# Three edits in an attention stage: a shorter second search update, side work tied to places of a turn, and unread matmuls where a place is empty

## The chip, the cores and the metric

The kernel runs on one core of a Trainium2 chip. The core has TensorE (matmuls; PE in the profile, PEld for its weight loads), VectorE (DVE), ScalarE (ACT), GpSimd (POOL) and SyncE (SP, which here only issues transfers). The engines run side by side and wait for each other through semaphores; each works its own instructions in the order in which the program gave them. The metric is the device time of one execution, in microseconds (us).

## The reference, cut to what matters

The program is two layers of a small vision network on four images of 256 channels and 32 x 32 = 1024 positions. Layer 0 is an attention block and a mixture of experts, layer 1 a selective scan and a mixture of experts. The change touches the attention block alone:

```
qkv  = conv1x1(x, qkv_w, qkv_b)          # 8 heads, 16 + 16 + 32 channels
attn = einsum(q, k) * SCALE              # 1024 x 1024 scores per head
k    = floor(N * mean(sigmoid(...)))     # one number for the whole batch
attn = where(rank of a score in its row < k, attn, -inf)
out  = einsum(v, softmax(attn))
pe   = depthwise 3x3 convolution of v
x    = x + conv1x1(out + pe, proj_w, proj_b)
```

Only the k largest scores of a row take part in the softmax, so the kernel must find for each of the 4 x 8 x 1024 rows the value of its k-th largest score. It does so by a search: it guesses a threshold, counts how many scores lie under it, and moves the threshold.

## The kernel before, in words

**Halves and turns.** The work is cut into 64 halves: 4 images, 2 groups of 4 heads, 4 pairs of query tiles, 2 tiles of 128 queries. One half is 128 queries for four heads, so four rows of 1024 scores in each partition. Half i enters in turn i, and a half stays in work for some eight turns, so each turn works on several halves at once: h0 is the one that enters, h1 entered one turn before, h2 two, h3 three; `pair` is two finished halves that go through the softmax together. Nothing reorders the work: the instructions go to each engine exactly as `turn(i)` writes them.

**One turn.** In the order of the code: TensorE computes the second half of h0's scores (`scores(1)`, L526) and ScalarE copies the four score tiles out of PSUM (`take`, L534). TensorE computes scores again, transposed and with the dropped ones pushed down, for two key tiles of the pair (`weights(q)`, L637 and L642). VectorE reads out the seven largest scores under h3's threshold (`window`, L551 and L554; two rows now, two later) and does the first search update (`update`, L592 to L616), for h1 and h2. ScalarE counts all four rows of h0 at its first guess (L500). Place 0. ScalarE takes exponentials (`exps`, L650), TensorE multiplies with the values and with ones (`sums`, L660). ScalarE and VectorE count h1 (L500 and L504). Place 1. TensorE does `weights(q + 1)`. VectorE does the second search update, for h0 and h1. Both count h2 a last time. GpSimd writes h3's mask, four instructions `dr` (L584), of which the first is told to wait for the second update, and then `verify` (L573 to L578). Place 2. Exponentials again; h0 is counted. Place 3. `start(i + 1)` computes the first half of the next half's scores (`scores(0)`, L526). h1 is counted. TensorE does the second `sums`. Place 4.

**Buffers.** Score tiles and transposed score tiles share three PSUM buffers of two banks. The scores of a half lie in SBUF in two of eight buffers `s_n`, so ScalarE's copies of a new half wait until the mask `dr` of the half four turns older has read them. All side work of TensorE shares one PSUM bank, `m`, with one buffer (`bank`).

**Side work and places.** Everything else of an image goes into five places of a turn, the calls `beside(i)`: the q and k of the next head group with their statistics and first guesses (`Group.steps`, 12 chunks), the values (`values`, 4 chunks a group), the convolution and its projection (`rest`: 4 chunks `vp`, 4 x 3 chunks of three convolution products, 4 chunks `pp`) and the last projection (`finish`, 4 chunks). Each is a generator. It yields True when a chunk of TensorE's work is issued, and the place is then closed; the instruction that empties the bank `m` is issued when the generator is next called, and the next chunk follows in the same place. `todo` holds for each generator the turn from which it may run, the turn by which it must be done, and whether a chunk is open. An open one goes on first, otherwise the one that is due first. `due(i)`, called by `start(i)`, runs whatever must be done by turn i, at once, ahead of `scores(0)`. The `rest` of an image also issues on GpSimd: a memset of `vpad` and, ahead of the first convolution chunk of each channel half, nine products `diag` (L450), which the convolution's matmuls (L455) load as weights. The last chunk of a group is the moments `mo` (L381, L382); behind them stands a square root on GpSimd (`sd`, L391), and VectorE then writes the guesses (L400 to L405). `rest` loads the image a second time by one SyncE transfer of 1 MB (`x_res`, L463).

Image b has turns 16 b to 16 b + 15, and its side work runs from turn 16 b + 5 to 16 b + 23.

Of the kernel before, what the change touches and what calls it, by code (L numbers as in the profile page):

```python
# [17 lines left out]
ALU = mybir.AluOpType  # L18
# [34 lines left out]
def metaformer(ctx: ExitStack, tc: tile.TileContext, t: dict, out: bass.AP):  # L53
    nc = tc.nc

    cons = ctx.enter_context(tc.tile_pool(name="cons", bufs=1))
    ident = cons.tile([P, P], F32, tag="ident", name="ident")
# [5 lines left out]
    first = cons.tile([P, E], F32, tag="first", name="first")  # L63
# [117 lines left out]
    with ExitStack() as st:  # L181
        wp = st.enter_context(tc.tile_pool(name="a_w", bufs=1))

        wqk = load_rows(wp, "wqk", 4 * P)
# [36 lines left out]
        with tc.tile_pool(name="a_ln", bufs=2) as lp, \  # L221
                tc.tile_pool(name="a_lnp", bufs=4, space=PSUM) as psl:
            g1 = load(lp, "g1", [P, CT, P], t["g1"].rearrange("(c p) o -> p c o", p=P))
            for b in range(B):
# [3 lines left out]
                for h in range(NHALF):  # L228
                    gp = psl.tile([P, HALF], F32, tag="m", name="gp")
                    for c in range(CT):  # L230
                        nc.tensor.matmul(gp, g1[:, c, :], xn[b][:, c, ts(h, HALF)],
                                         start=(c == 0), stop=(c == CT - 1))
# [5 lines left out]
                    i = b * NHALF + h  # L238
# [66 lines left out]
        def bank(name):  # L305

            return ps1.tile([P, HALF], F32, tag="m", name=name)
# [283 lines left out]

        def update():  # L592

# [4 lines left out]
            br = bracket.rearrange("p e k n j -> p e k (n j)")  # L598
            t, u = st_[:, 0], st_[:, 1]
# [8 lines left out]
            fr = p2.tile([P, R], F32, tag="fr", name="fr", bufs=1)  # L608
            nc.vector.scalar_tensor_tensor(fr, br[:, 0, 1, :], aim, dd[:, 1, :], ALU.subtract, ALU.mult)
            nc.vector.tensor_tensor(fr, fr, dd[:, 0, :], ALU.mult)  # L610
            nc.vector.tensor_tensor(fr, br[:, 0, 0, :], fr, ALU.subtract)
            low = p2.tile([P, R], F32, tag="low", name="low", bufs=1)
# [66 lines left out]

        todo = [[0, 0, groups[0, 0].steps(), False], [0, 0, images[0].values(0), False]]  # L680
        for b in range(B):
            i = b * PER
            todo.append([i + 5, i + 8, groups[b, 1].steps(), False])
            todo.append([i + 8, i + 13, images[b].values(1), False])
            if b + 1 < B:
                todo.append([i + 13, i + 16, groups[b + 1, 0].steps(), False])
                todo.append([i + 16, i + 21, images[b + 1].values(0), False])
            todo.append([i + 9, i + 20, images[b].rest(), False])
            todo.append([i + 21, i + 23, images[b].finish(), False])

        def beside(i):

            while True:
                ready = [w for w in todo if w[0] <= i]
                if not ready:
                    return
                w = next((w for w in ready if w[3]), None) or min(ready, key=lambda w: w[1])
                try:
                    w[3] = next(w[2])
                except StopIteration:  # L700
                    todo.remove(w)
                    w[3] = False
                if w[3]:
                    return
# [11 lines left out]
        def turn(i):  # L716
# [16 lines left out]
            if half(1) or half(2):  # L733
                to_u(slice(0, 2), FIRST_DVE[1])
                update()
            if h2:
# [3 lines left out]
            if h0:  # L740
                h0.count(4, h0.at_guess)
            beside(i)
            if pair:
# [6 lines left out]
            if h1:  # L750
                h1.count(FIRST_DVE[0], h1.at_state)
            beside(i)
            if pair:
# [13 lines left out]
            beside(i)  # L767
# [4 lines left out]
            beside(i)  # L772
            if i + 1 < len(order):
# [3 lines left out]
            if pair:  # L777
                pair.sums(q + 1)
            beside(i)

# [830 lines left out]
```

## Time and profile before

| | us |
|---|---|
| median of 3 runs (lowest, highest) | 4864.83 (4861.07, 4874.88) |
| profiled execution, and its span | 4900.55, 4898.8 |
| attention stage within the span | about 130 to 2120 |
| busy there: TensorE, VectorE, ScalarE, GpSimd | 1481.34, 1606.06, 1621.85, 915.86 |
| granted TensorE clock there, of full speed | 0.76 |

Below, a turn runs from ScalarE's first copy of a half's scores (L534, four copies a turn, 256 in all) to that of the next. Turn 0 starts at 140.2 us in the span. The turns of the second image and the first ones of the third, which repeat from image to image almost to a tenth:

| turns | starts at | length of each, us |
|---|---|---|
| 21 to 24 | 711.0 | 27.4, 31.0, 36.5, 31.1 |
| 25 to 28 | 837.1 | 31.6, 31.2, 35.6, 31.7 |
| 29, 30 | 967.2 | 30.4, 28.3 |
| 31, 32 | 1025.8 | 29.2, 29.5 |
| 33 to 36 | 1084.4 | 25.2, 26.7, 26.1, 26.7 |

Turns 17 to 20, 33 to 36, 49 to 52 and 62, 63 hold no side work at all.

How to read the profile's rows: a line of the timeline is the start in us from the span's start, the duration, the engine, the line of the kernel, the operation, the tile written and the tiles read, the shapes, and how many alike follow each other; in brackets how long the engine had been idle and what ended that. A line of groups ends with the total, the mean in ns and the idle time ahead. A matmul of f32 data shows as two entries.

### The profile page before, as it was taken

What the parts mean: (1) busy time and instruction counts of PE and PEld (TensorE: products, weight loads), DVE (VectorE), ACT (ScalarE), POOL (GpSimd) and SP (SyncE); (2) the same over time, 40 slices, a digit from 0 to 9 for tenths busy, and PEclk for the clock granted to TensorE, in tenths of its full rate; (3) what the DMA queues carried; (4) which work ended last, traced back from release to release, by engine and by line L of the source; (5) the groups of instructions that cost most, each with busy time, mean ns of one, the idle gap of its engine ahead of it and who ended that gap; (6) DMA issues with size and microseconds to landing.
All of it is one profiled execution on the core that took longest, in us unless ns stands there. A gap on an engine that the chain in (4) does not pass through costs nothing.

```text
span 4898.8 us, 51450 instructions
## 1 busy us (share of the span) xinstructions
PE 4004.6 (82%) x18714; PEld 2228.5 (45%) x18714; DVE 3255.5 (66%) x5263; ACT 2894.4 (59%) x3813; POOL 1405.0 (29%) x1126
## 2 busy tenths in 40 slices
PE   7378777877787777689999799989989994599993
PEld 4143434343434343356666333434433432488882
DVE  2687897789778887732223799999999995111212
ACT  3788898788878978522111666677666762122221
POOL 0244444545445454510000122222222223200004
PEclk8578767877797678778999899999999997799995
DMA  3000000000000000010000223323323334334433
GB/s 128 0 1 9 1 1 1 9 1 1 1 9 1 1 1 9 1 36 1 0 1 3 78 92 112 103 87 112 104 86 112 112 111 146 118 115 121 119 109 107
DMA packets 128616, 264.86 MB, mean 54 GB/s; under 512 B 29017, under 2 KB 77282, under 8 KB 127586
## 3 DMA queue, kind: packets, MB, share of 16 engines
q1 hardware_dynamic: 118144, 243.15, 15.3%
q0 software_dynamic: 6144, 16.79, 1.1%
q8 instruction: 150, 2.46, 0.2%
q10 hardware_dynamic: 4066, 1.55, 0.1%
q14 instruction: 112, 0.92, 0.1%
HBM read 224.74 MB, written 36.70 MB: 53 GB/s over the span
## 4 chain that ended last, share of the span: by engine, by line
PE 29%; DVE 19%; issue 3%; SPq 2%; ACT 2%; DMA 1%; POOL 0%; another core or an unknown queue 0%; ACTq 0%; DVEq 0%; POOLq 0%
PE hp L1505 6%; PE yp L1511 6%; PE y L1012 5%; PE hp L1005 5%; DVE h L1284 4%; DVE h L1269 4%; DVE h L1260 4%; PE hp L1255 3%; DVE yc L1294 2%; SPq L1478 2%; DVE h L1278 1%; PE y L1295 1%; PE hp L1288 1%; ACT da_c L1242 0%; PE y L173 0%
## 5 line engine op out<-in xcount | busy, mean ns | idle before, releaser
L584 POOL TENSOR_SCALAR dr<-s_n,last 128x1024 bf16<-128x1024 f32 x256 | 724.6, 2848 | 955.2 <-DVE state L616 598.7
L1240 POOL TENSOR_TENSOR uu<-dx,bb 128x1024 f32<-128x1024 f32 x128 | 317.4, 2480 | 1521.3 <-issue 807.9
L500 ACT ACTIVATE junk_a<-s_n,state 128x1024 int8<-128x1024 f32 x448 | 514.1, 1148 | 21.7 <-DVE state L616 11.7
L1255 PE MATMUL hp<-h,ident 128*128 128x512 f32 x1024 | 496.9, 608 | 27.3 <-DVE h L1278 19.0
L1242 ACT ACTIVATE da_c<-delta,a_log 128x1024 f32<-128x1024 f32 x128 | 270.0, 2109 | 307.1 <-DVE h L1284 307.1
L504 DVE TENSOR_SCALAR_CACHE_REDUCE junk_v<-s_n,state 128x1024 int8<-128x1024 f32 x320 | 408.6, 1277 | 8.0
L1507 ACT ACTIVATE hid<-hp,b 128x256 f32<-128x256 f32 x312 | 145.1, 473 | 415.4 <-PE hp L1505 415.4
L534 ACT COPY s_n<-sp 128x1024 f32<-128x1024 f32 x256 | 246.4, 1014 | 227.0 <-PE sp L526 166.8
L551 DVE SCALAR_TENSOR_TENSOR w<-s_n,win 128x1024 f32<-128x1024 f32 x256 | 359.3, 1403 | 5.5
L1014 DVE SCALAR_TENSOR_TENSOR acc<-y,tk_comb,acc 128x256 f32<-128x256 f32 x256 | 121.0, 484 | 356.0 <-PE y L1012 352.1
L660 PE MATMUL o_ps<-ex,vT 128*32 128x256 f32 x2048 | 274.1, 490 | 83.8 <-ACT ex L650 81.0
L1514 DVE TENSOR_TENSOR ys<-yp,b2e 128x512 f32<-128x512 f32 x39 | 27.0, 692 | 467.4 <-PE yp L1511 467.4
L1255 PEld LDWEIGHTS hp<-h,ident 128*128 128x128 f32 x1024 | 191.3, 193 | 304.3 <-issue 202.5
L554 DVE MAX8 win<-w 128x8 f32<-128x1024 f32 x256 | 314.5, 1228 | 8.8
L1255 PE MATMUL hp<-h,twice 128*128 128x512 f32 x512 | 258.8, 625 | 64.1 <-DVE h L1260 40.6
L500 ACT ACTIVATE junk_a<-s_n,guess 128x1024 int8<-128x1024 f32 x256 | 295.0, 1152 | 6.2
L1260 DVE TENSOR_TENSOR_SCAN h<-da,uu 128x1024 f32<-128x1024 f32 x128 | 290.1, 2266 | 3.6 <-ACT da L1248 3.6
L1284 DVE TENSOR_TENSOR_SCAN h<-da_c,uu 128x1024 f32<-128x1024 f32 x128 | 292.3, 2284 | 0.0
L1007 ACT ACTIVATE hid<-hp,b 128x512 f32<-128x512 f32 x128 | 88.0, 687 | 345.6 <-PE hp L1005 344.8
L1269 DVE TENSOR_TENSOR_SCAN h<-da,uu 128x1024 f32<-128x1024 f32 x128 | 289.9, 2264 | 0.0
L1505 PE MATMUL hp<-xe,w 128*128 128x256 f32 x1248 | 280.8, 383 | 7.5 <-DVE xe L1498 7.5
L650 ACT ACTIVATE ex<-sT 128x1024 f32<-128x1024 f32 x256 | 246.4, 1012 | 63.1 <-PE sT L642 62.7
(480 smaller groups left out, 8147.7 us busy)
## 6 DMA issues: line engine op xcount, KB each, us to landing
bb<-bc_d SPq DMA_DIRECT2D x128, 512.0 KB, 4.8
cb<-bc_d SPq DMA_DIRECT2D x128, 512.0 KB, 4.0
w<-in_w SPq DMA_DIRECT2D x47, 1024.0 KB, 5.0
slots_x<-zeros SPq DMA_DIRECT2D x1, 9984.0 KB, 32.4
xs<-slots_x SPq DMA_DIRECT2D x39, 256.0 KB, 3.1
slots_y<-ys SPq DMA_DIRECT2D x39, 256.0 KB, 2.4
b2e<-in_b SPq DMA_DIRECT2D x39, 128.0 KB, 3.8
x_in<-in_x SPq DMA_DIRECT2D x4, 1024.0 KB, 7.9
```

Source lines behind the costliest of these rows:

```text
L500: nc.scalar.activation(junk, self.row(r), AF.Sign, bias=thr, scale=-1.0, accum_out=u)
L504: nc.vector.tensor_scalar(junk, self.row(r), thr, None, ALU.is_lt, ALU.add, accum_out=u)
L551: nc.vector.scalar_tensor_tensor(w, self.row(r), self.win[:, r, 0:1], self.row(r), ALU.is_gt if r < LAST_DVE else ALU.is_ge, ALU.subtract, ...
L554: nc.vector.max(out=self.win[:, r, 1:], in_=w)
L584: ins = nc.gpsimd.tensor_scalar(dr, self.row(r), self.last[:, r : r + 1], None, ALU.is_lt)
L1240: nc.gpsimd.tensor_tensor(self.uu[:, 0], self.prep.dx[:, c], self.bb, ALU.mult)
L1255: nc.tensor.matmul(self.hp[h], ident if eye is None else eye, view[:, ts(h, HW // NHALF), :], start=first, stop=False)
L1260: nc.vector.tensor_tensor_scan(rows.rearrange("p r w -> p (r w)"), self.da, self.uu[:, 0], 0.0, ALU.mult, ALU.add)
L1269: nc.vector.tensor_tensor_scan(hs[:, ::-1], self.da[:, ::-1], self.uu[:, 0][:, ::-1], 0.0, ALU.mult, ALU.add)
L1284: nc.vector.tensor_tensor_scan(hs, self.da_c, self.uu[:, 1], 0.0, ALU.mult, ALU.add)
L1505: nc.tensor.matmul(hp[:, f % 2], w1[:, c, ts(f, P)], xe[:, c], start=(c == 0), stop=(c == CT - 1))
L1511: nc.tensor.matmul(yp[:, a], hid[:, f, ts(a, P)], w2e[:, f, :], start=(f == 0), stop=(f == NF - 1))
```

## The change

First, `update` gets an argument. The call near the start of a turn passes `stay=True` and does what it did. The call in the middle passes `stay=False`: it leaves out the two comparisons that find the rows whose count is already near the aim (L613, L615) and the predicated copy that spares those rows (L616), and writes the new threshold of every row by the subtraction.

Second, a start is now given in places, five to a turn, and a generator may be limited to some places: the groups to places 1 to 4, from place 2 of one turn earlier than before; the convolution and its projection (`rest`) to places 1 and 3. A chunk that is open goes on in any place.

Third, where a place of the first 64 turns has nothing to start, `keep_awake` issues matmuls of the identity with a weight matrix into a fresh tile of the bank `m`: two in place 0, one elsewhere. Nothing reads them.

```diff
-        def update():
+        def update(stay):
...
+            if not stay:
+                return nc.vector.tensor_tensor(t, br[:, 0, 0, :], fr, ALU.subtract)
             nc.vector.tensor_tensor(fr, br[:, 0, 0, :], fr, ALU.subtract)
...
-        todo = [[0, 0, groups[0, 0].steps(), False], [0, 0, images[0].values(0), False]]
+        PLACES = 5
+        todo = []
+
+        def plan(first, needed, steps, places=range(PLACES)):
+            todo.append([first, needed, steps, False, places])
+
+        plan(0, 0, groups[0, 0].steps())
+        plan(0, 0, images[0].values(0))
         for b in range(B):
             i = b * PER
-            todo.append([i + 5, i + 8, groups[b, 1].steps(), False])
-            todo.append([i + 8, i + 13, images[b].values(1), False])
+            plan((i + 4) * PLACES + 2, i + 8, groups[b, 1].steps(), (1, 2, 3, 4))
+            plan((i + 8) * PLACES, i + 13, images[b].values(1))
             if b + 1 < B:
-                todo.append([i + 13, i + 16, groups[b + 1, 0].steps(), False])
-                todo.append([i + 16, i + 21, images[b + 1].values(0), False])
-            todo.append([i + 9, i + 20, images[b].rest(), False])
-            todo.append([i + 21, i + 23, images[b].finish(), False])
-
-        def beside(i):
+                plan((i + 12) * PLACES + 2, i + 16, groups[b + 1, 0].steps(), (1, 2, 3, 4))
+                plan((i + 16) * PLACES, i + 21, images[b + 1].values(0))
+            plan((i + 9) * PLACES, i + 20, images[b].rest(), (1, 3))
+            plan((i + 21) * PLACES, i + 23, images[b].finish())
+
+        def keep_awake(count):
+            junk = bank("junk_p")
+            for _ in range(count):
+                nc.tensor.matmul(junk, ident, wqk[:, 0, :], start=True, stop=True)
+
+        def beside(i, place=None):
             while True:
-                ready = [w for w in todo if w[0] <= i]
-                if not ready:
+                ready = [w for w in todo if w[0] <= i * PLACES + (place or 0) and (place is None or place in w[4])]
+                w = next((w for w in todo if w[3]), None) or min(ready, key=lambda w: w[1], default=None)
+                if w is None:
+                    if place is not None and i < len(order):
+                        keep_awake(2 if place == 0 else 1)
                     return
-                w = next((w for w in ready if w[3]), None) or min(ready, key=lambda w: w[1])
...
-                update()
+                update(stay=True)
...
-            beside(i)
+            beside(i, 0)
...
-            after = update() if h0 or h1 else None
+            after = update(stay=False) if h0 or h1 else None
```

The other four calls of `beside` pass 1, 2, 3 and 4. Read through by hand, the new rules give for the turns 21 to 36 these chunks; `e` is the emptying of the bank by ScalarE or VectorE, J1 and J2 are unread products, and `due` is what `start` runs ahead of `scores(0)`:

| turn | place 0 | 1 | 2 | 3 | 4 |
|---|---|---|---|---|---|
| 21 | e, finish | e, finish | e, finish | e, finish | e, qp |
| 22 | e, J2 | ktp | e, ktp | e, mp | e, mq |
| 23 | e, J2 | mq | e, mo | mo | due: sd, guess, vtp; vtp |
| 24 | e, vtp | vtp | e, J1 | J1 | J1 |
| 25, 26 | J2 | vp | e, J1 | vp | e, J1 |
| 27 | J2 | conv | conv | conv | e, J1 |
| 28 | J2 | conv | conv | conv | e, qp |
| 29 | e, J2 | qp | e, qp | e, qp | e, ktp |
| 30 | e, J2 | ktp | e, mp | e, mq | e, mq |
| 31 | e, J2 | mo | mo | sd | due: guess, diag, conv; conv |
| 32 | conv | e, conv | conv | conv | e, vtp |
| 33 | vtp | e, pp | e, vtp | vtp | e, J1 |
| 34 | J2 | pp | e, J1 | pp | e, J1 |
| 35 | J2 | pp | e, J1 | J1 | J1 |
| 36 | J2 | J1 | qp | e, qp | e, qp |

The other images are alike, except that the last has no next group: its twelve convolution chunks stand in turns 59 to 62, in places 1 to 3. In all 177 unread products are issued.

More of the change, by code (lines that the diff above doesn't have):

```diff
@@ L751, in turn @@
                 h1.count(FIRST_DVE[0], h1.at_state)
-            beside(i)
+            beside(i, 1)
             if pair:
@@ L766, in turn @@
                     pairs[h3.i // 2] = Pair(halves[h3.i - 1 : h3.i + 1], images[h3.b])
-            beside(i)
+            beside(i, 2)
             if pair:
@@ L771, in turn @@
                 h0.count(FIRST_DVE[1], h0.at_state)
-            beside(i)
+            beside(i, 3)
             if i + 1 < len(order):
@@ L778, in turn @@
                 pair.sums(q + 1)
-            beside(i)
+            beside(i, 4)
         with tc.manual_schedule():
```

## The prediction

> **What bounds the kernel now.** First the stage view of 130 to 2120 us (columns: PE, PEld, DVE, ACT and POOL busy, then granted clock): no engine is full, and ScalarE (1621.85 of 1990) and VectorE (1606.06) are nearly equal. So waits decide, and ScalarE's waits come next (waiter, what it waited for, total, times, longest).
>
> ```profile
> 130.00:2120.00 1990.00, 1481.34 (x10559) 760.66 (x10559) 1606.06 (x3393) 1621.85 (x2414) 915.86 (x725) 0.76 0.02 5
> ...
> ACT s_n L534 <- PE sp L526: 166.8, 55, 7.0
> ACT ex L650 <- PE sT L642: 62.7, 24, 6.9
> ACT s_n L534 <- POOL dr L584: 58.0, 32, 3.7
> ```
>
> The largest wait is for scores that stand on TensorE behind side work: in turn 27, three convolution products ahead of `scores(1)`.
>
> ```profile
> 901.55 2.84 PE L455 MATMUL ap__6501<-vpad,diag 128*128 128x512 f32 x6
> ...
> 904.32 1.14 PE L526 MATMUL sp<-k__5278,q 16*128 16x512 f32 x8
> ...
> 905.49 2.84 ACT L534 COPY s_n<-sp 128x1024 f32<-128x1024 f32 x3 [4.61 <-PE sp L526]
> ```
>
> Turn 34 has no side work. There the mask holds ScalarE: the update ends, four `dr` run for 11.3 us, and the copies wait for the last. `scores(1)` is done by then.
>
> ```profile
> 1127.89 0.17 DVE L616 COPY_PREDICATED state<-move,fr 128x8 f32<-128x8 int32 x1
> ...
> 1128.26 11.30 POOL L584 TENSOR_SCALAR dr<-s_n,last 128x1024 bf16<-128x1024 f32 x4 [13.24 <-DVE state L616]
> ...
> 1134.46 2.08 PE L526 MATMUL sp<-k__7127,q 16*128 16x512 f32 x4
> ...
> 1136.33 1.90 ACT L534 COPY s_n<-sp 128x1024 f32<-128x1024 f32 x2
> ...
> 1139.59 1.93 ACT L534 COPY s_n<-sp 128x1024 f32<-128x1024 f32 x2 [1.35 <-POOL dr L584]
> ```
>
> Last, two places where GpSimd's order counts. `diag` and `sd` that are issued after the mask start only behind it and `verify`:
>
> ```profile
> 870.92 6.95 POOL L450 TENSOR_SCALAR diag<-ident,pe_w 128x128 f32<-128x128 f32 x9
> ...
> 871.58 2.84 PE L455 MATMUL ap__6310<-vpad,diag 128*128 128x512 f32 x6 [1.07 <-POOL diag L450]
> ...
> 804.23 5.44 POOL L391 TENSOR_TENSOR sd<-sd,half 128x32 f32<-128x32 f32 x1
> ...
> 809.70 0.25 DVE L400 SCALAR_TENSOR_TENSOR guess<-sd,z,mo 128x32 f32<-128x32 f32 x1 [6.97 <-POOL sd L391]
> ```
>
> **ScalarE's own turn** is the yardstick: in turn 34, 26.7 us less its 1.92 us wait for `dr`, so 24.8 us without side work. I add emptyings (0.67 us each with a 0.07 gap) and waits. As a check, turn 27 before: 24.8 + two emptyings 1.5 + waits 4.6 and 1.7, and 3.3 at the next turn's first copy: 35.9, against 35.6.
>
> **The shorter update** takes away L613, L615 and L616, 261 + 229 + 175 ns; at turn 34 the end of the update moves from 1128.06 to 1127.45, 0.6 us. Over 65 turns that is 40 us of VectorE, and on the path only where ScalarE waits for `dr`: the empty turns, 26.2 on average, become 25.6. Elsewhere ScalarE or TensorE ends last. Over turns 18 to 20, 34 to 36 and 50 to 52 it is -3.4 net of the projection now put there. Ends: 0, and 0.6 in all turns, -40; I stay near the first, since 32 short waits for `dr` are all there is to shorten.
>
> **The convolution's four turns** (25 to 28 and their like) lose the chunks ahead of `scores`. What remains is place 4: ScalarE empties the bank last in its turn, and the next product waits for that and stands ahead of `scores(1)`, which the second copy waits for. The wait is the product, plus 1.15 for the scores, plus 0.15 of handing over, less 1.0 for the first copy. An unread product has the shape of a convolution product: 2.84 / 3 = 0.95 us at full clock, and 1.5 where those ran cold (4.54 for three at 914.01). So 1.25 us with J1 and some 2.8 with a qp chunk (1.95); cold, 2.8 with J1. TensorE's queue in turn 27: fixed work 10.5 us at full clock, three chunks 8.5, J2 and J1 2.9, 22 in a turn of 27, so the chunks in places 1 to 3 hide behind counts (3.8, 3.7 and 5.0 us of ScalarE) but leave `scores(1)` 0.6 late. Turns 25 to 28 become 26.3, 27.7, 27.5 and 27.4: 108.9 for 130.1. For the four images 437 for 514.6: -78.
>
> **Turns 4 to 8 and 21 to 24.** The first fall from 145.1 to 136. In the later three sets mp and mq move one turn forward, so VectorE's 4.3 us wait for mp goes, but `sd` still stands behind the mask: mask 11.3, `verify` 1.7, `sd` 5.4, guess 1.4 and then VectorE's counts and windows to the first update, 10.5 us, which ScalarE's count waits for. 123 for 126 each. Together -17. Turns 13 and 14 and their like: +1.2 each, +4, the qp and ktp of place 4.
>
> **The collision in turns 15, 31 and 47** is the step against the change. Before, `sd` stood in place 1, ahead of the mask. Now it stands in place 3, and `due` puts the guess, the second channel half's `diag` and a convolution chunk ahead of `scores(0)`. From the start of turn 31: second update ends at 19.3, mask 30.6, `verify` 32.3, `sd` 37.8, first `diag` 38.5. TensorE, idle since 22, starts the convolution cold, 5.1 us, then `scores(0)`, first copy at 45.4 instead of about 27; then `sums`, the chunk in place 4, `scores(1)`: second copy at 52, counts at 55. From there before's turn 24 needed 24.3 us to its end. So turns 31 and 32 take 80 instead of 58.6, and turn 33, with vtp behind an emptying and a pp chunk, 29.2 instead of 25.2: +25 a time, three times, +75. Neither `diag` nor `sd` has other cover; the last image has no such turn. Ends: 0, if the chunk hid as in turn 25, and 35, if turn 32 also runs cold throughout.
>
> **Moved and free.** `vpad`'s memset (2.02 us) stays ahead of the mask with GpSimd idle; without that cover the mask would be 2 late. The `x_res` transfer starts when the convolution ends, turn 32, and its first reader is in turn 33, place 2, over 20 us later; SyncE has nothing else queued. J products in places 0 to 3 hide under the exponentials and counts: in turn 34 TensorE is busy 19 of 26.7 us; uncovered, each would cost 1 to 1.5. In empty turns J1 of place 4 is hidden: `sums` end at 1134.5, and the second copy needs `scores(1)` at 1137.3. Turns 0 to 3, 61, 62 and the tail, where two pp chunks spill: about 0.
>
> **Sum:** -78 - 17 + 4 + 75 - 3 = -19 us on the profiled 4900.6, so 4881.6. That execution is 0.7% above the median of the runs; the same 0.4% off 4864.8 gives 4846.
>
> **The clock.** In the window 1112.1 to 1125.7 the granted clock was 0.50 although TensorE was busy for 8.59 us and its longest gap was 2.9. [...] By the rows, turn 26 with 25.2 us busy of 31.2 ran at 1.00, so I take the filled turns as warm.
>
> **Rivals.** (1) *Place 4 costs more*, the slower case. 33 turns have ScalarE empty the bank in place 4 with a product behind it. Cold throughout, each costs 1.5 us more: +50, 4896. For: the half clock in turn 34, and turn 28's cold chunk (4.2 us). Against: turn 26. It decides from 19 / 33 = 0.6 us a turn, and is measurable from 1.0. (2) *No collision*: the convolution of turn 31 hides, three times 20 us come back, 4786. For: in turn 25 the chunk waited 1 us for `diag`. Against: there no `sd` stood between. (3) *The two cancel*: a collision of 31 each, or convolution turns of 28.5, brings 4865. For: two large terms of opposite sign. Also possible: the change doesn't raise the clock at all; then it is rival 1.
>
> **How the numbers follow.** Forecast (-15 to -50, own range 4815 to 4850) 0.40; rival 1 0.20; rival 2 0.13; rival 3 0.27. 0.3%, 15 us, is what a measurement of this kernel can tell. Faster is the forecast and rival 2, 0.53; same 0.27; slower 0.20. The range 4798 to 4888 leaves out rival 2 and the worse half of rival 1's chance, bounded by the collision's ends (15 to 31 each) and 0.8 us a turn in place 4.
>
> **What would show it.** Turns 27 and its like near 27.5 us; ScalarE's wait for sp well under 167 outside turns 16, 32 and 48, and there 15 to 25 us each, behind `diag`; waits for `dr` falling; granted clock of the stage near 0.9 or more; 65 fewer L613 entries. I am wrong if the collision is far from 25, or if place 4 costs over 2 us with one unread product.

## The result, and the profile after

The changed kernel takes **4888.85 us** (median of 4 runs, 4884.46 to 4891.17) against 4865.09 (4 runs, 4861.07 to 4874.88) for the kernel before on the same chip: a ratio of 1.0045, 95% interval 1.0027 to 1.0062. It is slower by 24 us, where I forecast 19 faster with a range of 4798 to 4888. The sign is wrong and the time lies just outside the range.

The profiled execution after took 4891.17 us (span 4889.5). Its attention stage, from the first copy of scores to the first instruction of the next stage, takes 1983.1 us. The kernel before takes 1962.2 there in the execution shown above and 1964.9 in a second one, so the loss of 18 to 21 us lies in this stage. (The spans of the two first profiles differ the other way round, 4898.8 to 4889.5. That comes from later stages, some 30 us longer in that one execution of the kernel before and not in its second one, which took 4871.29 us.)

First the stage view of 130 to 2120 us of the kernel after (busy PE, PEld, DVE, ACT, POOL, granted clock), then its waits (waiter, what it waited for, total, times, longest).

```profile
130.00:2120.00 1990.00, 1545.25 (x10843) 749.51 (x10843) 1551.14 (x3184) 1620.44 (x2408) 924.00 (x724) 0.81 0.01 3
...
ACT s_n L534 <- PE sp L526: 221.6, 76, 16.9
...
DVE guess L400 <- POOL sd L391: 69.0, 7, 11.0
...
ACT s_n L534 <- POOL dr L584: 11.7, 9, 3.6
```

TensorE is busier by 64 us, VectorE less busy by 55, and the granted clock went from 0.76 to 0.81. ScalarE hardly waits for the mask any more (58.0 before, 11.7 now), but waits longer for scores (166.8 before, 221.6 now): one wait has taken the place of another. VectorE's wait for `sd` has doubled (33.0 before).

The convolution's turns did what they should. The start of turn 27 in the timeline of the kernel after:

```profile
908.11 0.67 ACT L443 ACTIVATE vpad<-vp,bv_col 128x512 f32<-128x512 f32 x1
908.68 1.00 ACT L534 COPY s_n<-sp 128x1024 f32<-128x1024 f32 x1
...
908.83 1.13 PE L705 MATMUL junk_p<-wqk,ident 128*128 128x512 f32 x2 [1.25 <-ACT vpad L443]
...
909.89 1.14 PE L526 MATMUL sp<-k__5008,q 16*128 16x512 f32 x8
...
911.06 2.84 ACT L534 COPY s_n<-sp 128x1024 f32<-128x1024 f32 x3 [1.39 <-PE sp L526]
```

Three convolution products and a wait of 4.61 us stood here before. Now ScalarE empties the bank, one unread product follows, and the second copy waits 1.39 us.

The collision came as described: `sd` and the nine `diag` behind the mask and `verify`, TensorE idle for 13 us, and the copy of turn 32 behind all of it.

```profile
1041.78 11.30 POOL L584 TENSOR_SCALAR dr<-s_n,last 128x1024 bf16<-128x1024 f32 x4 [13.96 <-DVE state L612]
...
1054.63 5.44 POOL L391 TENSOR_TENSOR sd<-sd,half 128x32 f32<-128x32 f32 x1
1060.06 6.04 POOL L450 TENSOR_SCALAR diag<-ident,pe_w 128x128 f32<-128x128 f32 x9
1060.10 0.36 DVE L400 SCALAR_TENSOR_TENSOR guess<-sd,z,mo 128x32 f32<-128x32 f32 x1 [10.99 <-POOL sd L391]
...
1060.73 5.42 PE L455 MATMUL ap__7745<-vpad,diag 128*128 128x512 f32 x6 [13.03 <-POOL diag L450]
...
1066.08 1.14 PE L526 MATMUL sp<-k__7011,q 16*128 16x512 f32 x8
...
1067.31 1.01 ACT L534 COPY s_n<-sp 128x1024 f32<-128x1024 f32 x1 [16.85 <-PE sp L526]
```

In an empty turn the kernel before waited for `dr`. Turn 36 of the kernel after shows what is there now: the sums end, the unread product of place 4 runs, then the scores, and the second copy waits 2.02 us for them.

```profile
1180.65 0.99 ACT L534 COPY s_n<-sp 128x1024 f32<-128x1024 f32 x1
...
1180.89 0.61 PE L662 MATMUL o_ps<-ex,ones 128*32 128x256 f32 x8
...
1181.44 1.12 PE L705 MATMUL junk_p<-wqk,ident 128*128 128x512 f32 x2
...
1182.49 1.14 PE L526 MATMUL sp<-k__7011,q 16*128 16x512 f32 x8
1183.67 2.84 ACT L534 COPY s_n<-sp 128x1024 f32<-128x1024 f32 x3 [2.02 <-PE sp L526]
```

The lengths of the turns, summed by groups, place the loss (us; measured is after less the first profile of before):

| turns | before, two profiles | after | predicted | measured |
|---|---|---|---|---|
| 0 to 3 | 78.6, 78.6 | 75.8 | about 0 | -2.8 |
| 4 to 8 | 145.1, 145.1 | 148.9 | -9 | +3.8 |
| 21 to 24 and their like | 376.8, 378.1 | 386.5 | -8 | +9.7 |
| convolution, four times four | 514.6, 513.9 | 443.7 | -78 | -70.9 |
| 13, 14 and their like | 176.0, 177.5 | 177.8 | +4 | +1.8 |
| 15 to 17 and their like | 252.3, 251.2 | 315.6 | +75 | +63.3 |
| 18 to 20 and their like | 238.0, 238.6 | 252.7 | -3 | +14.7 |
| 61 to the end of the stage | 180.8, 181.9 | 182.2 | about 0 | +1.4 |
| sum | 1962.2, 1964.9 | 1983.1 | -19 | +20.9 |

The two large terms hold to within 12 us each and together give -8, where they were predicted to give -3. They belong together: half of the convolution's chunks and its projection left the four turns for turns 31 to 35 and their like, so the -71 holds work that has moved. The miss of 40 is in the small ones: the groups' turns (4 to 8, 21 to 24) by 30, turns 18 to 20 by 18; all other lines give back 8.

### The profile page after: what moved, and what is told of

It is laid out like the page before. It is cut to its first block, busy times and chain, and to the rows that moved or that the text cites. A ratio compares the mean times of both kernels' runs of the same rounds, so it can differ in the third digit from the quotient of the medians.

```text
span 4889.5 us, 51952 instructions
## 1 busy us (share of the span) xinstructions
PE 4075.9 (83%) x19068; PEld 2220.5 (45%) x19068; DVE 3207.5 (66%) x5068; ACT 2897.3 (59%) x3813; POOL 1414.4 (29%) x1126
## 5 line engine op out<-in xcount | busy, mean ns | idle before, releaser
L1525 ACT ACTIVATE hid<-hp,b 128x256 f32<-128x256 f32 x312 | 145.1, 473 | 415.3 <-PE hp L1523 415.3
L534 ACT COPY s_n<-sp 128x1024 f32<-128x1024 f32 x256 | 246.8, 1015 | 241.9 <-PE sp L526 221.6
L551 DVE SCALAR_TENSOR_TENSOR w<-s_n,win 128x1024 f32<-128x1024 f32 x256 | 348.6, 1362 | 5.4
L705 PE MATMUL junk_p<-wqk,ident 128*128 128x512 f32 x354 | 257.2, 846 | 87.5 <-ACT vpad L443 18.0
L662 PE MATMUL o_ps<-ex,vT 128*32 128x256 f32 x2048 | 237.3, 448 | 74.4 <-ACT ex L652 68.4
```

The costliest lines, as they stand in the source:

```text
L551: nc.vector.scalar_tensor_tensor(w, self.row(r), self.win[:, r, 0:1], self.row(r), ALU.is_gt if r < LAST_DVE else ALU.is_ge, ALU.subtract, ...
```

## The experiments

After the two traces my **theory** was: the collision eats what the convolution's places bring; the unread products bring little, because those in place 4 stand ahead of scores; the shorter update brings little. The **rivals**: the unread products are the loss by themselves; the shorter update is worth much more than its waits show and something hides it; the groups' new places, not the collision, are the loss. Ratios are always to the kernel before on the same chip. Its median was 4874.12 us in the first batch, 4893.97 in the second and 4873.95 in the third, so ratios, and not times, are compared across batches. Times in brackets are ranges, ratios in brackets 95% intervals.

### The kernel before once more

No edit, one profile, to learn how much one profiled execution differs from the next.

> The kernel before once more, for a second profiled execution. If the extra 28 us behind the attention stage in the first one (627, 106 and 98 us for three stretches in which the changed kernel took 616, 100 and 87) belong to that execution alone, this one has the shorter stretches, with attention again at 1962 us. If they belong to the kernel, it has the longer ones again.

Measured: 4871.29 us, attention stage 1964.9, every group of turns within 1.5 us of the first profile. What the table above shows beyond that is the change.

### The shorter second update alone

The kernel before with the new argument of `update`, and nothing else.

```diff
-        def update():
+        def update(stay):
...
+            if not stay:
+                return nc.vector.tensor_tensor(t, br[:, 0, 0, :], fr, ALU.subtract)
...
-                update()
+                update(stay=True)
...
-            after = update() if h0 or h1 else None
+            after = update(stay=False) if h0 or h1 else None
```

> The kernel before with the shorter second update alone. Theory that VectorE is off the path but for the mask: only turns in which ScalarE waits for dr gain, up to 0.6 us each, some 20 to 30 turns, so -10 to -18 us (4848 to 4855), and the waits of the copies for dr fall from 58 to about 40 us. Rival, VectorE bounds every turn: 65 turns at 0.6 us, -40 us (4825). Rival, nothing: the next limit takes it over, within 5 us of before.

Measured: 4850.02 us (4848.51 to 4856.14), ratio 0.9955 [0.9941, 0.9968]: **24 us faster**, more than the theory's 10 to 18 and less than the rival's 40. Two waits of ScalarE in the second profile of the kernel before:

```profile
ACT s_n L534 <- PE sp L526: 162.7, 54, 7.4
...
ACT s_n L534 <- POOL dr L584: 57.4, 34, 3.7
```

and in the kernel with the shorter update:

```profile
ACT s_n L534 <- PE sp L526: 152.0, 55, 6.4
...
ACT s_n L534 <- POOL dr L584: 47.1, 27, 3.6
```

The wait for `dr`, where I had put the whole gain, falls by 10. The wait for scores falls by 11 as well. The empty turns 18 to 20 and their like, where the mask is waited for, shorten by 5, but so do others: the convolution's, where it is hardly waited for, by 8, and turns 21 to 24 and their like by 9. The three instructions take 0.665 us of VectorE, 43 over 65 turns, and more than half of it comes through. By which chain it reaches the convolution's turns I did not trace.

### The change without its unread products

```diff
-                    if place is not None and i < len(order):
-                        keep_awake(2 if place == 0 else 1)
```

> The changed kernel without any unread product. Theory that the products in place 4 hold scores(1) behind an emptying of the bank: without them the turns that end with an emptying lose a wait of 1.2 to 1.4 us in some 25 turns, -25 to -35 us against the changed kernel (4855 to 4865). Rival, the products keep TensorE's clock up and that is worth more: the granted clock of the attention stage falls from 0.81 to under 0.75 and the time rises by 10 to 50 us (4900 to 4940). Rival, the two cancel: within 10 us of 4889.

Measured: 4894.05 us (4878.48 to 4895.95), ratio 1.0041 [1.0026, 1.0056], where the change itself has 1.0045. The 177 products are worth nothing in sum, to within some 0.2%, although they do raise the clock: 0.75 without them, 0.81 with them.

### The change without the collision

The first group of the next image may again use all places, so its last chunk no longer comes after the mask of turn 31.

```diff
-                plan((i + 12) * PLACES + 2, i + 16, groups[b + 1, 0].steps(), (1, 2, 3, 4))
+                plan((i + 12) * PLACES + 2, i + 16, groups[b + 1, 0].steps())
```

> The changed kernel, but the first group of the next image may use place 0 too. That puts its square root sd into place 0 of turns 15, 31 and 47, ahead of the mask, and the second channel half's diag and first convolution chunk into place 1. Theory that these three stretches are where the change loses: turns 15 to 17 and their like fall from 316 us in all to about 250, and the kernel to 4822 to 4840, faster than before. Rival, the loss lies with the groups' other chunks, late emptyings and a cold TensorE: the three stretches fall, but turns 13, 14 and 18 to 20 take most of it, 4870 to 4885.

Measured: 4838.08 us (4836.75 to 4840.16), ratio 0.9926 [0.9911, 0.9941]. Against the change that is 1.2%, 58 us. In the profile turns 15 to 17 and their like fall from 315.6 to 264.6, so 51 of it is there. The collision was the largest single loss.

### The same without any unread product

The edits of the last two together, to price the products where no collision covers them.

```diff
-                plan((i + 12) * PLACES + 2, i + 16, groups[b + 1, 0].steps(), (1, 2, 3, 4))
+                plan((i + 12) * PLACES + 2, i + 16, groups[b + 1, 0].steps())
...
-                    if place is not None and i < len(order):
-                        keep_awake(2 if place == 0 else 1)
```

> The changed kernel with the first group of the next image allowed in place 0 (no collision), without unread products. Theory that the products' gain by the clock and their cost in place 4 cancel, as in the pair with the collision: within 8 us of 4838. Rival, they cost: 4818 to 4828. Rival, they help once the collision is gone, since TensorE is then nearer to the path: 4850 or more.

Measured: 4854.33 us (4849.36 to 4860.27), ratio 0.9922 [0.9901, 0.9942]; clock 0.76. The same ratio as with all of them, on a different chip. So the products cancel without the collision as well.

### Unread products in places 0 to 3 only

Without the collision, and `keep_awake` is not called in place 4.

```diff
-                    if place is not None and i < len(order):
+                    if place not in (None, 4) and i < len(order):
```

> The same, with unread products in places 0 to 3 but none in place 4. Theory that place 4 is where they cost and the other places where they help: each of some 17 turns that end with an emptying and one product loses its wait of 1.4 us, -15 to -25, 4813 to 4823. Rival, the product's wait there is covered by what comes next (the copies wait for dr or VectorE is late): within 6 us of 4838. Rival, without it the scores run at half clock and cost more than the product: 4844 or more.

Measured: 4808.74 us (4807.61 to 4811.96), ratio **0.9827** [0.9808, 0.9845]. This splits the zero into two parts. The 128 products in places 0 to 3 bring 0.95% (46 us, against the kernel with none), with clock 0.81 for 0.76. The 40 in place 4 cost 1.0% (48 us, against the kernel with all, in the other batch): 1.2 us each, and two to three times what was expected. Turn 20 shows how one acts. First the timeline of the kernel after, then that of this kernel:

```profile
691.22 1.12 PE L705 MATMUL junk_p<-wqk,ident 128*128 128x512 f32 x2
...
692.28 1.14 PE L526 MATMUL sp<-k__3108,q 16*128 16x512 f32 x8
...
693.45 2.84 ACT L534 COPY s_n<-sp 128x1024 f32<-128x1024 f32 x3 [3.67 <-PE sp L526]
```

```profile
665.90 2.07 PE L526 MATMUL sp<-k__3090,q 16*128 16x512 f32 x8
...
667.08 1.01 ACT L534 COPY s_n<-sp 128x1024 f32<-128x1024 f32 x1 [0.29 <-PE sp L526]
...
670.28 1.93 ACT L534 COPY s_n<-sp 128x1024 f32<-128x1024 f32 x2 [2.19 <-POOL dr L584]
```

With the product ScalarE waits 3.67 us for scores. Without it the wait is 0.29, although the eight entries take 2.07 us here instead of 1.14, and the mask is what comes late next: 2.19. The kernel after differs from this one in the collision too. In the kernel that differs only in place 4's products the wait is 2.91, and turn 20 is 30.8 us long in both: here the mask takes over all of the gain. The time comes from other turns: summed over the stage, the convolution's fall by 13, turns 15 to 17 and their like by 11, 21 to 24 and their like by 7, 13 and 14 and their like by 7, 18 and 19 and their like by 6, while turns 4 to 8 rise by 6.

### The change with the collision, without products in place 4

The edit of the last experiment on the changed kernel, to see whether that price also holds in the change itself.

```diff
-                    if place is not None and i < len(order):
+                    if place not in (None, 4) and i < len(order):
```

> The changed kernel whose only edit is that place 4 of a turn never gets an unread product; places 0 to 3 keep theirs and the collision of turns 15 to 17 stays. Theory A, an unread product in place 4 stands ahead of scores(1) and costs about 1.4 us wherever one is issued (34 turns, some 48 us, as the pair of kernels without the collision showed: ratio 0.9922 or 0.9926 with or without all products, 0.9827 without those of place 4): ratio to the kernel before 0.9945 to 0.996 instead of 1.0045, ScalarE's wait for sp in the stage falls from 221.6 to about 175. Rival B, the collision hides most of it: ratio 1.000 to 1.003.

Measured: 4867.31 us (4854.31 to 4879.37), ratio 0.9983 [0.9971, 0.9995]; ScalarE's wait for scores 175.0. The gain is 0.62% (30 us for 34 products, 0.9 us each), between the two expectations: the wait fell as far as foreseen, the time only by two thirds. In the profile the convolution's turns fall by 16 and turns 18 to 20 by 9, while turns 15 to 17 (+1) and 21 to 24 (-1) don't move, unlike without the collision (-11 and -7). My reading is that GpSimd ends last there, so that TensorE's delay costs nothing; it is not shown by a run of its own.

### `diag` one convolution earlier

The collision has two parts, `sd` and `diag`. Here the second channel half's nine products are issued on GpSimd at the end of the last chunk of the first half, a chunk before they are needed.

```diff
-                for c in range(CT):
-                    diag = wk.tile([P, 9, P], F32, tag="diag", name="diag")
+                def make_diag(c):
+                    d = wk.tile([P, 9, P], F32, tag="diag", name="diag")
...
+                    return d
+
+                diag = make_diag(0)
+                for c in range(CT):
...
+                        if h == NHALF - 1 and c + 1 < CT:
+                            diag = make_diag(c + 1)
```

> The changed kernel, with the nine diag of the second channel half issued one convolution earlier, at the end of turns 12, 28 and 44, so that in turns 15, 31 and 47 TensorE's convolution chunk no longer waits for GpSimd; sd and the guess stay late. Theory that the collision has two parts, TensorE behind diag and VectorE behind sd: scores(0) comes on time, but ScalarE's count waits for the first update behind the guess, so turns 31 and 32 take about 65 us instead of 75.7; the three stretches fall by 30 us and the kernel to 4855 to 4865. Rival, diag alone: the stretches fall by 55 or more, 4830 to 4840. Rival, sd alone: under 10 us, 4880 or more.

Measured: 4880.63 us (4872.93 to 4885.58), ratio 0.9967 [0.9958, 0.9977], 0.8% less than the change. Turns 15 to 17 and their like fall from 315.6 to 286.6. Turn 31 in this kernel's timeline:

```profile
1038.24 4.95 PE L459 MATMUL ap__7745<-vpad,diag 128*128 128x512 f32 x6 [0.32 <-DVE mo L386]
...
1043.12 1.14 PE L532 MATMUL sp<-k__7021,q 16*128 16x512 f32 x8
...
1044.35 1.01 ACT L540 COPY s_n<-sp 128x1024 f32<-128x1024 f32 x1 [3.67 <-PE sp L532]
...
1044.88 5.45 POOL L391 TENSOR_TENSOR sd<-sd,half 128x32 f32<-128x32 f32 x1
...
1050.36 0.25 DVE L400 SCALAR_TENSOR_TENSOR guess<-sd,z,mo 128x32 f32<-128x32 f32 x1 [11.02 <-POOL sd L391]
```

The convolution starts without waiting for GpSimd, cold (4.95 us for six entries, where turn 27 of the kernel before took 2.84), and the first copy waits 3.67 instead of 16.85. But `sd` is still behind the mask, and VectorE still waits 11 us for it. So without `diag` behind the mask 29 of the 63 us are gone. That does not make the other 34 the price of `sd` alone; the next experiment shows that the two overlap.

### The groups where they were before

The change, with both groups' start and places as in the kernel before.

```diff
-            plan((i + 4) * PLACES + 2, i + 8, groups[b, 1].steps(), (1, 2, 3, 4))
+            plan((i + 5) * PLACES, i + 8, groups[b, 1].steps())
...
-                plan((i + 12) * PLACES + 2, i + 16, groups[b + 1, 0].steps(), (1, 2, 3, 4))
+                plan((i + 13) * PLACES, i + 16, groups[b + 1, 0].steps())
```

> The changed kernel with the head groups started where they were before (turns 5 and 13 of an image, any place); the convolution's places, the shorter update and the unread products stay. Theory that the groups' chunks are the second loss: turns 4 to 8, 20 to 24 and 18 to 20 return to the values with the shorter update alone (143, 369 and 233 us in all instead of 149, 387 and 253), and sd stands ahead of the mask again, while diag is still behind it in place 3 of turns 15, 31 and 47; so -44 and some -30, 4810 to 4825. Rival, the groups' rows are slow because unread products and chunks share place 4 in every plan: those turns stay within 10 us of the changed kernel's and only the collision's part falls, 4845 to 4860.

Measured: 4861.24 us (4857.06 to 4868.76), ratio 0.9929 [0.9910, 0.9948], 1.2% less than the change. Turns 4 to 8: 142.9 (148.9 in the change); 21 to 24 and their like 372.3 (386.5); 18 to 20 and their like 238.9 (252.7); 15 to 17 only from 315.6 to 309.1, since `diag` still falls behind the mask there. In turn 31 `sd` now starts ahead of the mask, and the first copy of the next turn still waits 14.47 us for scores that stand behind `diag` (16.85 in the change). So the collision's two parts run side by side. Over the kernel before, these turns lose 63 us with both behind the mask, 57 with `diag` alone, 34 with `sd` alone and 12 with neither (the experiment without the collision). So some 34 us of the change are the second group's earlier start and its places, in turns in which I had forecast a gain.

### The best of these, with the second group where it was

No collision, no products in place 4, and the second group again from turn 5 in all places.

```diff
-            plan((i + 4) * PLACES + 2, i + 8, groups[b, 1].steps(), (1, 2, 3, 4))
+            plan((i + 5) * PLACES, i + 8, groups[b, 1].steps())
```

> The kernel without the collision and without products in place 4 (ratio 0.9827), and in addition the second group of an image starts again in turn 5 of the image, all places, as in the kernel before. Theory A, the group's early start and its places were what lengthened turns 4 to 8 (151.5 us there, 142.9 with the old start) and 21 to 24 (374.6 over three sets, against 368.8): turns 4 to 8 about 143, turns 21 to 24 and their like about 367 to 372, in all 10 to 18 us less: ratio 0.979 to 0.9805. Rival B, with no product in place 4 the places no longer matter: within 0.15% of 0.9827.

Measured: 4782.36 us (4775.71 to 4788.73), ratio 0.9809 [0.9793, 0.9826]. The profile has turns 4 to 8 at 142.8 (151.5 with the change's start), 21 to 24 and their like at 371.4 (374.6), 18 to 20 and their like at 237.4 (245.3). These three groups move as in the last experiment, by 20 us in all instead of 34; turns 13 to 17 and their like give 12 back (13, 14: 179.4 for 171.6; 15 to 17: 257.3 for 253.2). The ratios alone, 0.9809 and 0.9827, have intervals that overlap.

### The second group still earlier, with `sd` ahead of the mask

As in the kernel without collision and place 4, but the second group may start in place 1 of turn 4, in all places; the tiles for q and k are taken only after its first chunk.

```diff
-            plan((i + 4) * PLACES + 2, i + 8, groups[b, 1].steps(), (1, 2, 3, 4))
+            plan((i + 4) * PLACES + 1, i + 8, groups[b, 1].steps())
...
-                self.q = wk.tile([P, L], F32, tag="q", name="q", bufs=2)
-                self.k = wk.tile([P, L], F32, tag="k", name="k_", bufs=2)
...
+                        if name == "q" and h == 0:
+                            self.q = wk.tile([P, L], F32, tag="q", name="q", bufs=2)
+                            self.k = wk.tile([P, L], F32, tag="k", name="k_", bufs=2)
```

> As the kernel without the collision and without products in place 4, but the second group of an image starts in place 1 of turn 4, in all places, so that its square root sd is issued in place 1 of turn 23 (39, 55), ahead of the mask. Theory A, sd behind the mask is what VectorE waits for in turn 24 (9.8 to 11 us): turns 21 to 24 and their like fall by 7 to 10 us a set, 374.6 to about 350, ratio 0.975 to 0.978. Rival B, the chunks now in places 0 and 4 cost what sd brings: turns 21 to 24 stay at 370 to 380, ratio 0.981 to 0.985.

Measured: 4767.87 us (4767.00 to 4772.29), ratio **0.9784** [0.9767, 0.9800], the fastest of all. Turns 21 to 24 and their like take 341.4 us; before they took 376.8, in the change 386.5. The mask starts in the change's turn 23, `sd` comes behind it and `verify` in turn 24, VectorE waits 11 us for it and ScalarE's count waits for the guess:

```profile
806.85 11.30 POOL L584 TENSOR_SCALAR dr<-s_n,last 128x1024 bf16<-128x1024 f32 x4 [19.64 <-DVE state L612]
...
819.48 0.26 POOL L578 TENSOR_TENSOR fine<-fine,sure 128x36 f32<-128x36 f32 x1
819.70 5.44 POOL L391 TENSOR_TENSOR sd<-sd,half 128x32 f32<-128x32 f32 x1
...
825.17 0.25 DVE L400 SCALAR_TENSOR_TENSOR guess<-sd,z,mo 128x32 f32<-128x32 f32 x1 [11.00 <-POOL sd L391]
...
825.52 1.15 ACT L500 ACTIVATE junk_a<-s_n,guess 128x1024 int8<-128x1024 f32 x1 [0.40 <-DVE guess L400]
```

In turn 23 of this kernel `sd` stands ahead of the mask's first `dr`, with GpSimd idle before it, and VectorE waits 1.4:

```profile
777.25 5.46 POOL L393 TENSOR_TENSOR sd<-sd,half 128x32 f32<-128x32 f32 x1 [9.57 <-DVE sd L392]
...
782.70 11.30 POOL L586 TENSOR_SCALAR dr<-s_n,last 128x1024 bf16<-128x1024 f32 x4
782.75 1.11 DVE L402 SCALAR_TENSOR_TENSOR guess<-sd,z,mo 128x32 f32<-128x32 f32 x1 [1.43 <-POOL sd L393]
```

The mask is later for it by a few us, and that costs far less. The group's other chunks move forward with `sd`, so the 33 us are what the whole move brings. A few us come back in turns 13 and 14 (179.9 for 171.6) and 15 to 17 (258.9 for 253.2). The sum of the stage falls by 25.7.

### The convolution in all places again

As in the kernel without collision and place 4, but `rest` may run in every place. This prices the convolution's places by themselves.

```diff
-            plan((i + 9) * PLACES, i + 20, images[b].rest(), (1, 3))
+            plan((i + 9) * PLACES, i + 20, images[b].rest())
```

> As the kernel without the collision and without products in place 4, but the convolution and its projection run in all five places again, as in the kernel before. It prices the convolution's places by themselves. Theory A, the chunks of three products ahead of scores in places 0 and 4 are what made the four convolution turns long: 427.9 us over the four images goes back to about 500, of which emptier turns 18 to 20 and 34 to 36 give back some 10: ratio 0.993 to 0.998. Rival B, the shorter update and the unread products made those turns short and the places did little: convolution turns at 440 to 460, ratio 0.984 to 0.988.

Measured: 4917.08 us (4913.09 to 4919.36), ratio 1.0092 [1.0075, 1.0109], against 0.9827 with the places. That is 2.7%, some 130 us, more than expected. The convolution's turns rise from 427.9 to 519.3, by 91 us; turns 13 and 14 by 15 and 15 to 17 by 23, where the displaced group's `sd` falls behind the mask again. The start of turn 27 of this kernel, to be put beside that of the changed kernel above:

```profile
911.01 5.42 PE L455 MATMUL ap__6465<-vpad,diag 128*128 128x512 f32 x12 [1.30 <-ACT x L460]
...
916.36 1.14 PE L526 MATMUL sp<-k__4978,q 16*128 16x512 f32 x8
...
917.63 0.99 ACT L534 COPY s_n<-sp 128x1024 f32<-128x1024 f32 x1
...
919.29 2.84 PE L455 MATMUL ap__6465<-vpad,diag 128*128 128x512 f32 x6
...
922.06 1.14 PE L526 MATMUL sp<-k__4978,q 16*128 16x512 f32 x8
...
923.24 2.84 ACT L534 COPY s_n<-sp 128x1024 f32<-128x1024 f32 x3 [4.61 <-PE sp L526]
```

The convolution chunk of place 4 is back ahead of the second half's scores, and the wait is the same 4.61 us as in the kernel before.

## Why the prediction was wrong, point by point

**The convolution's four turns: right.** -78 predicted, -70.9 measured. The wait of 1.4 us in place 4 of turns 26 and 27 is the 1.25 worked out there. Turn 25 was missed, 30.2 us for 26.3, with a wait of 4.28 for scores; 26 to 28 came within 0.8. The wait behind a qp chunk, put at 2.8, is 2.25 by the prediction's own terms (1.95 + 1.15 + 0.15 - 1.0), and turns 29 and 45 show 2.25. The places by themselves, priced in the last experiment, are the largest gain of the change.

**The collision: right in place, cause and nearly in size.** +75 predicted, +63.3 measured. Turns 31 and 32 take 44.2 and 31.4, together 75.7 for 80; the wait behind `diag` lay within the 15 to 25 us named. Turn 33 takes 30.1 for 29.2. Taking it away brings 1.2% and 51 of the 63 us; the other 12 are not `sd` or `diag` behind the mask, and these turns then still hold convolution chunks that the four turns had before. Both parts are shown, and they overlap: 29 come back without `diag` behind the mask, 6 with only `sd` taken from there.

**"Turns 4 to 8 and 21 to 24", -17: the first step that failed,** by 30 us. For turns 4 to 8 the prediction named no term behind its 9 us. For the later sets it named one, "VectorE's 4.3 us wait for mp goes". It moved with `mp`. In the change VectorE waits 4.8 us for it in turn 22, and over the stage 18.6 in seven waits, against 11.2 in three in the second profile of the kernel before. The product now comes in place 3 of turn 22 instead of place 0 of turn 23, behind the same emptying, and is waited for all the same.

The wait for `sd` grew too, from 7.0 to 11.0, but it is not what made these turns longer. The kernel before started that mask here, and its guess at 809.70:

```profile
791.38 11.30 POOL L584 TENSOR_SCALAR dr<-s_n,last 128x1024 bf16<-128x1024 f32 x4 [17.02 <-DVE state L616]
```

In both kernels the guess starts 18.3 us behind the mask's start (806.85 and 825.17 in the change). VectorE only waits for `sd` what it waited for the moments `mo` before (1.5 us now, 5.4 then); the two waits together are 12.5 and 12.4. Of the stage's 69.0 us for `sd`, against 33.0, the collisions hold 33.0 and turns 24, 40 and 56 hold 30.6, against 20.4. Over the three sets turns 23 and 24 together even fell, from 200.5 to 195.0, while 21 rose from 82.1 to 92.4 and 22 from 94.2 to 99.1. Turn 21 shows what the sum had at nothing. The qp chunk of turn 20's place 4 stands ahead of the scores; ScalarE empties it behind its counts, and `finish`, which found the bank free before, waits for that and is waited for by VectorE:

```profile
724.70 1.98 PE L343 MATMUL qp<-x,wqk 128*128 128x512 f32 x4
...
727.78 2.84 ACT L534 COPY s_n<-sp 128x1024 f32<-128x1024 f32 x3 [5.47 <-PE sp L526]
...
736.30 3.78 PE L481 MATMUL pp<-att,wproj 128*128 128x512 f32 x4 [4.11 <-ACT k__5008 L350]
...
740.12 0.69 DVE L484 TENSOR_TENSOR x<-pp,x_res 128x512 f32<-128x512 f32 x1 [5.86 <-PE pp L481]
```

In the first profile of the kernel before, the copies of turn 21 waited 1.35 us, for the mask, and VectorE did not wait for `finish` there. With the groups back in their places turns 4 to 8 and 21 to 24 are 20 us shorter. With `sd` ahead of the mask 21 to 24 are 33 shorter than in the nearest kernel, but `sd` was behind it in the kernel before as well: that is a gain left lying, not a loss of the change.

**"Turns 18 to 20", -3: the second step,** by 18 us. Turns 20, 36 and 52 hold nearly all of it: 32.5, 29.9 and 32.3 for 26.7 each. I had credited turns 21 to 24 with the group's earlier start and put its first chunks in turn 20 at nothing. ScalarE empties two of them (0.67 us each) and waits 1.5 for one that ran cold (3.78 us at a granted clock of 0.50; 1.94 at 1.00), and at the turn's start its second copy waits longer for scores (the 3.67 us above, 1.00 before). With the second group back in its place turn 20 and its like are 13 shorter over the three sets. Turn 4, the first image's like of turn 20, rose from 25.2 to 29.1. Turns 20 to 24 have to be summed as one stretch.

**"In empty turns J1 of place 4 is hidden": the third step.** I read from before's turn 34 that the sums end 2.8 us ahead of the copy's need. I forgot that the scores come between, 2.08 us at a granted clock of 0.50 in that turn, which leaves 0.7 for a product of 1.1 or more. The runs put it at 0.9 us each in the change (34 products) and 1.2 without the collision (40). In the change's profile 9 us of that lie in turns 18 to 20 and their like, which had it at nothing, and 16 in the convolution's turns, where the sum had priced it. Rival 1 said that place 4 decides from 0.6 us a turn: it does, but not by running cold throughout, as that rival had it.

**The shorter update, -3: mis-sized.** 24 alone. I had allowed it only where ScalarE waits for `dr`, and set 40 as the far end. How much of the 24 survives beside the other parts was not measured.

**The clock.** "Near 0.9 or more" fell: 0.81 over the stage. It did rise in the filled turns of the second image (from 0.86 to 0.94 over turns 25 to 28), but not in those of the third (0.86 and 0.85 over 41 to 44). The products bring 46 us in places 0 to 3, so filling gaps does buy time, as I had taken from the row of 1112.1 to 1125.7 (granted clock 0.50, longest gap 2.9 us). That it is the clock that brings it (0.81 for 0.76) is argued and not shown by itself. What I did not do is to separate what they bring from what one of them costs ahead of scores.

**The chances.** The forecast and rivals 2 and 3 don't hold. The sign is that of rival 1, and place 4 is in it, but most of the miss is the groups' turns, for which no rival stood: I had put 0.20 on slower because I looked for one mechanism, and it was several small terms that I had set at zero or below.

## What to carry to other kernels

Filler work on a throttled engine had two prices here, a gain that is spread over the stage (46 us) and a cost where the next thing in the queue is waited for (48 us); price the places apart, since they cancelled to nothing and one condition in the code separated them. When side work moves a turn earlier, sum the whole stretch that it leaves and enters, and ask of every wait that "goes" where its producer now stands. On an in-order engine with one long job a turn (here the mask of 11.3 us), it matters whether a short producer is issued ahead of it or behind it (VectorE waited 1.43 us for `sd` in the fastest kernel, ahead of the mask, and 11.00 in the change, behind it). Before calling a longer wait a loss, see whether the wait ahead of it has shrunk by as much.

## What the runs showed of the hardware

**The clock dropped behind gaps of 2.29 and of 1.10 us.** The stretches below, of the kernel after, have the start and end, the length, the busy times of PE, PEld, DVE, ACT and POOL, and then the granted clock.

```profile
680.24:683.65 3.41, 1.12 (x9) 0.47 (x6) 3.31 (x8) 3.38 (x6) 2.52 (x1) 1.00 0.00 0
683.65:690.48 6.83, 6.77 (x35) 2.04 (x38) 6.66 (x10) 6.04 (x10) 6.83 (x4) 0.50 0.00 0
690.48:697.31 6.83, 5.52 (x57) 2.65 (x50) 6.27 (x16) 3.86 (x5) 3.29 (x7) 1.00 0.00 0
697.31:700.72 3.41, 3.41 (x9) 1.28 (x6) 3.34 (x3) 3.31 (x7) 0.00 (x0) 0.50 0.00 0
```

In these 20 us the clock changed at 683.65, 690.48, 697.31 and 700.72, which lie 6.83, 6.83 and 3.41 us apart. In the first stretch TensorE was idle for 2.29 us of 3.41, and was then held at half for 6.83 us while it was busy for 6.77. In the third it was busy 5.52 of 6.83 with no gap over 1.10, and got half clock again for 3.41. Such gaps did not always go ahead of a drop: the next stretch, 700.72 to 714.37, opens with 3.41 us of which TensorE was busy for 1.93, with a gap of 1.19, and the clock stayed full through all of its 13.65 us. What sets the clock these rows do not show.

**A higher clock was not by itself a shorter time.** From no unread product to 168 the stage's clock rose from 0.76 to 0.82 and the ratio stayed (0.9922, 0.9926). With 128 of them the clock is 0.81 and the ratio 0.9827. The fastest kernel has 111 and a clock of 0.80.
